# Two banded layers on one core: band products in a two-bank tile, two of eight normalised columns on VectorE, and another order of the step

## The chip, the cores and the metric

The kernel runs on one core of one Trainium2 chip. The metric is device time in microseconds (us) of one execution, as the median of several runs. The engines are named as in the profile: PE is TensorE's matmul stream, PEld its weight loads, DVE is VectorE, ACT is ScalarE, POOL is GpSimd, and SP is SyncE, which issues the DMAs.

## The reference, cut to what matters

The input `x` is 512 x 512 x 64 in float32. Two layers of the same form run one after the other, each with its own weights:

```python
def _layer(x):                       # xn: group norm of x, then layer norm over the 64 channels
    left  = (xn @ Wl + bl) * mask * sigmoid(xn @ Wlg + blg)      # 64 -> 128 channels
    right = (xn @ Wr + br) * mask * sigmoid(xn @ Wrg + brg)
    out_gate = sigmoid(xn @ Wog + bog)
    out = _banded_ingoing(left, right, 4)    # out[i,j,h] = sum over |d|<=4 of left[i+d,i,h] * right[i+d,j,h]
    out = _ln(out, out_norm_scale, out_norm_bias) * out_gate     # layer norm over the 128 channels
    return x + out @ Wo + bo
```

The sum over the band is, for each of the 128 channels, a matrix product along the first image axis with a band matrix of width 9.

## The kernel before, in words

The 512 rows are cut into nine blocks of 64 rows with some overlap, and each block into two halves of the 512 columns. A **chunk** is one block with 128 columns from each half, and the 128 partitions hold 64 rows for each of the two column halves. A layer has 18 chunks of 16 **steps**. A step `t` handles eight columns per half: one `Unit` on the input side, and, some 30 steps later, one `Out` on the output side. `RO` holds the projected right side of the chunk, and later the band products in the same place.

What a step does, by engine (the names are the functions that the loop in `layer` calls, lines 800 to 910):

- POOL: `affine` (group norm, two operations on the tile `z`, `128x512`), `inner_norm(t+2)` (subtract the mean and multiply by the inverse deviation, again two operations on `z`), the twelve small operations of the inverse square root in `solve` (every fourth step), and `biased` (adds the bias to the residual rows in `XR`). How many units are put through `affine` in a step varies: over the steps 0 to 15 of a chunk it is 1, 1, 2, 1, 2, 1, 1, 2, 1, 1, 1, 0, 1, 1, 0, 0.
- DVE: `out_stats` (statistics `sto` of the band products, from none to seven a step), `inner_stats` (statistics `sti` of `z`), the five small operations that open `solve`, `right_end` twice (writes `RO` from the projection and its gate), `times_gate` twice (writes `ZH`), `ended` (adds the residual), and one copy of band products for each call of `mix`.
- ACT: `right_gate` twice (`sg`), `gated` (`gate`, two operations), `norm` (eight operations that write `on`, four and four), `kept` (writes `zT`, two operations), and one copy of band products for each `mix`.
- PE: `right` twice (16 matmul records each), `gates`, `turned` (transposes of `on`), `transposed` (transposes of the next unit's `z`), `end` (the last projection of the step before), `sums` (statistics for the next group norm, only in the first layer), and `mix`.

`mix` computes the band product of eight channels: 16 small matmul calls (32 records in the profile) in the four 64x64 tiles of the array. Steps 0 to 9 of a chunk hold 2, 1, 2, 2, 1, 2, 1, 2, 2, 1 calls, and steps 10 to 15 hold none. Each engine works in the order in which the program issues (`InOrder`), so the order of the calls in the loop is the order of each engine's queue.

PSUM is handed out from two rings. `two_banks()` gives tiles of two banks from a ring of two buffers (`ps2`): both `right`, and `transposed`. `one_bank()` gives single banks from a ring of three in the first layer and four in the second (`ps`, `ps_all`): `gates`, `turned`, `end`, and, before the change, both halves of `mix`. A tile can be written again only when all readers of its earlier content are done. The tile `on` has one buffer, so `norm(t+1)` writes behind `turned(t)`.

Two lines say where the transposes sit before the change:

```python
            for u in inputs(t + 1):
                transposed(u)          # third use of the ps2 ring in a step: the buffer of right(units[t], 0)
```

Of the kernel before, what the change touches and what calls it, by code (L numbers as in the profile page):

```python
# [11 lines left out]
ALU = mybir.AluOpType  # L12
# [4 lines left out]
P = 128  # L17
# [5 lines left out]
JU = 8  # L23
JQ = 4
NU = JC // JU
HB = 8
HA = 16
NA = 3
NB = 32
# [24 lines left out]
def last(v: bass.AP, n: int) -> bass.AP:  # L54

    p, c = v.shape
    return v.unsqueeze(2).broadcast_to([p, c, n])
# [22 lines left out]
def tile_two_banded_layers(  # L80
# [47 lines left out]
    def one_bank():  # L128
        return ps.tile([P, 512], F32, tag="ps", name="bank")
# [302 lines left out]
    def inner_stats(u: Unit, st: bass.AP, k: int):  # L432

        en.vector.bn_stats(st[:, k, :], u.z[:, 2 * k : 2 * k + 2, :].rearrange("p t c -> p c t"))

    def inner_norm(u: Unit):
        z = u.z.rearrange("p (k t) c -> p k t c", t=2)
        m = u.mean.unsqueeze(3).broadcast_to([P, JU // 2, 2, D])
        en.gpsimd.tensor_tensor(z, z, m, ALU.subtract)
        en.gpsimd.tensor_tensor(u.z, u.z, last(u.rs, D), ALU.mult)  # L440

    def transposed(u: Unit):

# [62 lines left out]
    def right(u: Unit, q: int, w: dict):  # L506
        u.pr[q] = crossed(u, q, w["right"]).rearrange("p e k h -> p (e k) h")

    def right_gate(u: Unit, q: int):
        u.sg[q] = wk.tile([P, JQ, H], F32, tag="sg", name="sg", bufs=2)  # L510
        en.scalar.activation(u.sg[q], u.pr[q][:, :, H:], AF.Sigmoid)
# [55 lines left out]
    def mix(c: int, A: bass.AP, h0: int) -> list:  # L567


        j0 = c % 2 * (JC - JW)  # L570
        q = HB // 4
        R = RO.rearrange("p (s h) j t -> p s h j t", s=2)[:, :, h0 // 4 : h0 // 4 + q, j0 : j0 + JC]
        L = A.rearrange("p (s h) i t -> p s h i t", s=2)[:, :, h0 % HA // 4 : h0 % HA // 4 + q]
        ph = [one_bank().rearrange("i (h t j) -> i h t j", h=q, t=2) for s in range(2)]
        for h in range(q):
            for t in range(2):
                for s in range(2):
                    for e in range(2):
                        part, to = (slice(n * S, (n + 1) * S) for n in (e, e ^ s))
                        en.tensor.matmul(  # L580
                            ph[s][to, h, t, :], lhsT=L[part, s, h, :, t], rhs=R[part, s, h, :, t],
                            start=True, stop=True,
                        )
        return [(R[:, s], ph[s].rearrange("i h t j -> i h j t")) for s in range(2)]

    class Out:

# [4 lines left out]
    def out_stats(o: Out, st: bass.AP, k: int):  # L592
        en.vector.bn_stats(
            st[:, k, :],
            RO[:, :, o.c + 2 * k : o.c + 2 * k + 2, :].rearrange("p h j t -> p h t j"),
        )
# [60 lines left out]
    def gated(o: Out):  # L657
        b = o.blk
        n = 2 * JQ * b.m
        g = gp.tile([H, 4 * JQ * (S - WIN)], F32, tag="gate", name="gate")  # L660
        for e, pg in enumerate(o.pg):
            en.scalar.activation(
                g[:, e * n : (e + 1) * n].rearrange("h (k p) -> h k p", p=b.m), pg, AF.Sigmoid
            )

        o.g = g[:, : 2 * n].rearrange("h (x n p) -> h n x p", n=2, p=b.m)
# [31 lines left out]
    def biased(o: Out, w: dict, stats: bool):  # L698
        n = S + o.blk.m
        f = o.xr[:n, :, 1 : 1 + 2 * D]  # L700
        add = fewer if stats and o.blk.m < S - WIN else w["add"]
        en.gpsimd.tensor_tensor(f, f, mid(add[:n], JU // 2), ALU.add)
# [36 lines left out]
    def layer(src: bass.AP, dst: bass.AP, w: dict, stats: bool, then=None):  # L739
# [36 lines left out]
        def inputs(t: int) -> list:  # L776
            return [d[t] for d in (units, lefts) if t in d]
# [22 lines left out]
        for t in range(min(loads), last_t + 3):  # L800
            if then and t == max(units) + 2:
                then()
            for u in loads.get(t, []):
                if u not in early:
                    load(src, u)
            if t + 1 in outs:
                fetch(src, outs[t + 1], w, t + 1)
            for c, h in slabs.get(t, []):
                A[c, h] = take_left(c // per, h)
            if t + 2 in outs:  # L810
                recall(outs[t + 2])

            looking = []
            for o, k in looks.get(t, []):
                if sto is None:
                    sto = sm.tile([P, NB // 2, 6], F32, tag="sto", name="sto"), []
                st, os = sto
                if k == 0:
                    os.append(o)
                n = (len(os) - 1) * (JU // 2)  # L820
                looking.append((o, st[:, n : n + JU // 2, :], k))

            mixing, mixed = mixes.get(t, []), []
            todo = []
            for at, u in inners.get(t, []):
                key = (at + 1) // 4
                if key not in sti:
                    sti[key] = sm.tile([P, 3 * NB // 4, 6], F32, tag="sti", name="sti", bufs=3), []
                st, us = sti[key]
                n = len(us) * (JU // 2)  # L830
                u.mean = st[:, n : n + JU // 2, 1::3]
                todo += [(u, st[:, n : n + JU // 2, :], k) for k in range(JU // 2)]
                us.append(u)

            if t in lefts:
                for q in range(0, min(JU, NEAR * JQ - lefts[t].near), JQ):
                    left(lefts[t], q, w)
            for v in looking[0:3]:
                out_stats(*v)
            for u in inputs(t + 2):  # L840
                inner_norm(u)
            if t in units:
                right(units[t], 0, w)
            if t in units:
                right_gate(units[t], 0)
            if t in outs:
                gates(outs[t], w)
            if t in units:
                right(units[t], JQ, w)
            for u in affines.pop(t, []):  # L850
                affine(u, en.vector if u.at < NU + 4 else en.gpsimd)
            if t % 4 == 0 and t > NU:
                then_affine = affines.pop(t + 1, [])
            for v in looking[3:5]:
                out_stats(*v)
            for v in looking[5:]:
                out_stats(*v)
            for v in todo:
                inner_stats(*v)
            if t % 4 == 0:  # L860
                st, us = sti.pop((t + 4) // 4, (None, []))
                so, os = sto or (None, [])
                sto = None
                if us or os:
                    solve(w, us, os, st, so)
            if t in outs:
                gated(outs[t])
            if t in units:
                right_end(units[t], 0)
            if t in outs:  # L870
                biased(outs[t], w, stats)
            if t in outs:
                turned(outs[t], w)
            if t in units:
                right_gate(units[t], JQ)
            for u in inputs(t + 1):
                transposed(u)
            if t in outs:
                times_gate(outs[t], w)
            for u in then_affine:  # L880
                affine(u, en.gpsimd)
            then_affine = []
            if t - 1 in outs:
                end(outs[t - 1], w)
            if t in units:
                right_end(units[t], JQ)
            if len(mixing) > 0:
                c, h0 = mixing[0]
                mixed.append(mix(c, A[c, h0 // HA], h0))
            if t + 1 in outs:  # L890
                norm(outs[t + 1], 0, 4)
            for u in inputs(t + 1):
                kept(u)
            if stats and t - 2 in outs:
                sums(outs[t - 2], t - 2 == first_t, t - 2 == last_t)
            if len(mixing) > 0:
                en.scalar.copy(*mixed[0][0])
            if t - 1 in outs:
                ended(dst, outs[t - 1])
            if t + 1 in outs:  # L900
                norm(outs[t + 1], 4, 8)
            if len(mixing) > 1:
                c, h0 = mixing[1]
                mixed.append(mix(c, A[c, h0 // HA], h0))
            if len(mixing) > 0:
                en.vector.tensor_copy(*mixed[0][1])
            if len(mixing) > 1:
                en.scalar.copy(*mixed[1][0])
            if len(mixing) > 1:
                en.vector.tensor_copy(*mixed[1][1])  # L910

# [135 lines left out]
```

## Time and profile before

| | |
|---|---|
| median of 3 runs | 4813.95 us (4808.51 to 4821.8) |
| profiled execution: its own time | 4808.51 us |
| its span, first to last instruction | 4806.5 us |
| mean granted TensorE clock | 0.948 |
| busy, share of the span | DVE 82%, PE 79%, POOL 79%, ACT 77% |
| steps with everything at work, first layer | 16 chunks between about 555 and 2397 us |
| the same, second layer | 16 chunks between about 2842 and 4681 us |

The start of the span is the pass for the first group norm's statistics, the stretch around 2500 to 2800 us is the change of layers, and the rest is the two long stretches of the table, in which the steps repeat with the period of a chunk. Shares over the whole span mix these stages, so the step is read from windows inside the long stretches. An operation's time in the listing is from its start to its end; on DVE and ACT the next operation starts some 0.09 us before the last one's end, so sums of work are made from start to start.

### The profile page before, as it was taken

What the parts mean: (1) busy time and instruction counts of PE and PEld (TensorE: products, weight loads), DVE (VectorE), ACT (ScalarE), POOL (GpSimd) and SP (SyncE); (2) the same over time, 40 slices, a digit from 0 to 9 for tenths busy, and PEclk for the clock granted to TensorE, in tenths of its full rate; (3) what the DMA queues carried; (4) which work ended last, traced back from release to release, by engine and by line L of the source; (5) the groups of instructions that cost most, each with busy time, mean ns of one, the idle gap of its engine ahead of it and who ended that gap; (6) DMA issues with size and microseconds to landing.
All of it is one profiled execution on the core that took longest, in us unless ns stands there. A gap on an engine that the chain in (4) does not pass through costs nothing. (4 is left out here: it accounts for less than half of the span.)

```text
span 4806.5 us, 193543 instructions
## 1 busy us (share of the span) xinstructions
PE 3796.6 (79%) x76306; PEld 3293.0 (69%) x76306; DVE 3929.9 (82%) x9635; ACT 3708.4 (77%) x8732; POOL 3817.1 (79%) x4739
## 2 busy tenths in 40 slices
PE   1025799989999999999985478888888888888888
PEld 0024688878888887888854467777777777777775
DVE  6954788888888888888867478888888888888887
ACT  0013689888888898989883268888888888888899
POOL 0035999999999999999734589999999999999964
PEclk9997999999999999999997689999999999999999
DMA  7859677777777777777763967777777777777876
GB/s 299 336 178 108 172 212 213 215 210 215 211 209 210 211 214 212 214 212 215 199 170 100 105 168 212 216 214 209 217 213 215 213 213 218 210 216 211 222 200 179
DMA packets 1437651, 983.63 MB, mean 205 GB/s; under 512 B 167202, under 2 KB 1284424, under 8 KB 1432392
## 3 DMA queue, kind: packets, MB, share of 16 engines
q1 hardware_dynamic: 1432064, 969.75, 73.6%
q8 instruction: 604, 9.90, 0.9%
q14 instruction: 303, 2.48, 0.2%
q10 hardware_dynamic: 4680, 1.50, 0.1%
HBM read 658.42 MB, written 312.46 MB: 202 GB/s over the span
## 5 line engine op out<-in xcount | busy, mean ns | idle before, releaser
L373 ACT ACTIVATE on<-RO,nm,rs 128x128 f32<-128x128 f32 x4608 | 1927.7, 496 | 15.3 <-PE bank L373 9.9
L373 PEld LDWEIGHTS banks<-pack,zT 64*128 64x128 f32 x18576 | 1251.3, 195 | 549.5 <-ACT zT L373 288.9
L373 PE MATMUL banks<-pack,zT 64*128 64x128 f32 x18576 | 1365.6, 289 | 272.8 <-ACT zT L373 222.6
L373 DVE TENSOR_TENSOR RO<-banks,sg 128x512 f32<-128x512 f32 (+1 forms) x1188 | 795.3, 673 | 228.3 <-POOL sg L373 116.2
L373 DVE SCALAR_TENSOR_TENSOR ZH<-bank,pack,gate 128x448 f32<-128x448 f32 (+1 forms) x1152 | 741.6, 685 | 173.3 <-PE bank L373 97.3
L373 ACT ACTIVATE sg<-banks 128x512 f32<-128x512 f32 (+1 forms) x1188 | 698.0, 589 | 188.6 <-PE banks L373 188.2
L373 DVE BATCH_NORM_STATS2 sto<-RO 128x6 f32<-128x256 f32 x2304 | 800.8, 411 | 3.7
L373 POOL TENSOR_TENSOR z<-z,gb 128x512 f32<-128x512 f32 x536 | 684.8, 1278 | 42.0
L373 PE MATMUL bank<-RO,A 64*64 64x128 f32 x18432 | 706.0, 292 | 3.9 <-ACT RO L373 2.4
L373 PE MATMUL bank<-pack,ZH 128*64 128x64 f32 x18432 | 694.6, 231 | 5.0 <-ACT gate L373 4.1
L373 POOL TENSOR_TENSOR z<-z,ga 128x512 f32<-128x512 f32 x536 | 685.6, 1279 | 3.2 <-DMA z<-mid_x 1.9
L373 POOL TENSOR_TENSOR z<-z,rs 128x512 f32<-128x512 f32 x586 | 619.3, 1057 | 46.0
L373 DVE COPY RO<-bank 128x512 f32<-128x512 f32 x576 | 398.4, 692 | 310.6 <-PE bank L373 307.3
L373 PEld LDWEIGHTS bank<-pack,ZH 128*64 128x64 f32 x18432 | 612.6, 143 | 47.3 <-ACT gate L373 8.5
L373 POOL TENSOR_TENSOR z<-z,sti 128x512 f32<-128x512 f32 x586 | 627.9, 1072 | 0.0
L373 PEld LDWEIGHTS bank<-RO,A 64*64 64x64 f32 x18432 | 582.0, 142 | 43.0 <-ACT RO L373 4.1
L373 ACT ACTIVATE gate<-bank 128x448 f32<-128x448 f32 (+1 forms) x1152 | 565.8, 545 | 34.5 <-PE bank L373 32.0
L373 ACT ACTIVATE zT<-banks 128x512 f32<-128x512 f32 (+1 forms) x1084 | 463.5, 481 | 139.6 <-PE banks L373 128.9
L373 PE MATMUL bank<-zg,pack 64*128 64x448 f32 (+1 forms) x2304 | 564.3, 556 | 4.6 <-DMA zg<-later 4.6
L373 ACT COPY RO<-bank 128x512 f32<-128x512 f32 x576 | 333.2, 579 | 282.3 <-PE bank L373 282.1
L373 PE MATMUL banks<-ident,z 64*128 64x64 f32 x4336 | 254.1, 233 | 359.2 <-DVE RO L373 336.9
L373 DVE BATCH_NORM_STATS2 sti<-z 128x6 f32<-128x128 f32 x2344 | 500.5, 280 | 15.2 <-POOL z L373 14.2
(144 smaller groups left out, 3908.6 us busy)
## 6 DMA issues: line engine op xcount, KB each, us to landing
later<-zT SPq DMA_DIRECT2D x576, 256.0 KB
A<-left_of SPq DMA_DIRECT2D x1152, 128.0 KB
zg<-later SPq DMA_DIRECT2D x576, 256.0 KB
z<-in_x_dram SPq DMA_DIRECT2D x576, 128.0 KB
z<-mid_x SPq DMA_DIRECT2D x576, 128.0 KB
gn_x<-in_x_dram SPq DMA_DIRECT2D x16, 4096.0 KB
XR<-in_x_dram SPq DMA_DIRECT2D x448, 112.0 KB
mid_x<-XR SPq DMA_DIRECT2D x448, 112.0 KB
```

The lines of the kernel that those rows point to most:

```text
L373: return lambda *a, **k: tc.keep_in_program_order(f(*a, **k))
```

## The change

Three things are changed. `mix` takes one tile of two banks in place of two tiles of one bank, with the same matmuls and the same copies. For units behind number 16, `inner_norm` on POOL handles six of the eight columns, and the new `inner_norm_v` does the other two on DVE, one `tensor_scalar` of `128x64` per column, which subtracts and multiplies at once with two per-partition scalars. And the calls of a step come in another order: by engine, before and after:

| engine | before | after |
|---|---|---|
| PE | right 0, gates, right 4, turned, transposed, end, mix, sums, mix | gates, right 0, right 4, turned, end, sums, transposed, mix, mix |
| ACT | right_gate, gated, right_gate, norm 0-4, kept, copy, norm 4-8, copy | gated, right_gate, right_gate, norm 0-4, kept, copy, copy, norm 4-8 |
| DVE | stats, solve, right_end, times_gate, right_end, ended, copy, copy | stats, solve, right_end, right_end, times_gate, inner_norm_v, ended, copy, copy |
| POOL | inner_norm, affine, solve, biased, affine of the next step | affine, inner_norm, solve, biased, affine of the next step |

```diff
+ZV = 2
...
     def inner_norm(u: Unit):
-        z = u.z.rearrange("p (k t) c -> p k t c", t=2)
-        m = u.mean.unsqueeze(3).broadcast_to([P, JU // 2, 2, D])
-        en.gpsimd.tensor_tensor(z, z, m, ALU.subtract)
-        en.gpsimd.tensor_tensor(u.z, u.z, last(u.rs, D), ALU.mult)
+        n = ZV if u.at > NU else 0
+        m = last(u.mean.rearrange("p k t -> p (k t)")[:, n:], D)
+        en.gpsimd.tensor_tensor(u.z[:, n:], u.z[:, n:], m, ALU.subtract)
+        en.gpsimd.tensor_tensor(u.z[:, n:], u.z[:, n:], last(u.rs[:, n:], D), ALU.mult)
+
+    def inner_norm_v(u: Unit):
+        for j in range(ZV if u.at > NU else 0):
+            en.vector.tensor_scalar(
+                u.z[:, j], u.z[:, j], u.mean[:, j // 2, j % 2 : j % 2 + 1], u.rs[:, j : j + 1],
+                ALU.subtract, ALU.mult,
+            )
...
-        ph = [one_bank().rearrange("i (h t j) -> i h t j", h=q, t=2) for s in range(2)]
+        pb = two_banks()
+        ph = pb.rearrange("i (s h t j) -> i s h t j", s=2, h=q, t=2)
...
-                            ph[s][to, h, t, :], lhsT=L[part, s, h, :, t], rhs=R[part, s, h, :, t],
+                            ph[to, s, h, t, :], lhsT=L[part, s, h, :, t], rhs=R[part, s, h, :, t],
```

The rest of the diff moves the calls in the loop of `layer` (lines 835 to 910), as in the table. The calls that issue DMAs (`fetch`, `take_left`, `recall`, `kept`, `ended`) keep their order on SP's queue.

More of the change, by code (lines that the diff above doesn't have):

```diff
@@ L580, in mix @@
                         en.tensor.matmul(
-                            ph[s][to, h, t, :], lhsT=L[part, s, h, :, t], rhs=R[part, s, h, :, t],
+                            ph[to, s, h, t, :], lhsT=L[part, s, h, :, t], rhs=R[part, s, h, :, t],
                             start=True, stop=True,
                         )
-        return [(R[:, s], ph[s].rearrange("i h t j -> i h j t")) for s in range(2)]
+        return [(R[:, s], ph[:, s].rearrange("i h t j -> i h j t")) for s in range(2)]
     class Out:
@@ L837, in layer @@
                     left(lefts[t], q, w)
[L838 to L845, printed above, removed]
             if t in outs:
@@ L848, in layer @@
             if t in units:
-                right(units[t], JQ, w)
+                right(units[t], 0, w)
             for u in affines.pop(t, []):
@@ L853, in layer @@
                 then_affine = affines.pop(t + 1, [])
-            for v in looking[3:5]:
+            if t in units:
+                right(units[t], JQ, w)
+            if t in outs:
+                gated(outs[t])
+            if t in units:
+                right_gate(units[t], 0)
+            for v in looking[0:2]:
                 out_stats(*v)
-            for v in looking[5:]:
+            for u in inputs(t + 2):
+                inner_norm(u)
+            for v in looking[2:5]:
                 out_stats(*v)
@@ L859, in layer @@
                 inner_stats(*v)
+            if t in outs:
+                turned(outs[t], w)
+            for v in looking[5:]:
+                out_stats(*v)
             if t % 4 == 0:
@@ L865, in layer @@
                     solve(w, us, os, st, so)
+            if t in units:
+                right_gate(units[t], JQ)
             if t in outs:
-                gated(outs[t])
+                biased(outs[t], w, stats)
             if t in units:
                 right_end(units[t], 0)
[L870 to L873, printed above, removed]
             if t in units:
-                right_gate(units[t], JQ)
-            for u in inputs(t + 1):
-                transposed(u)
+                right_end(units[t], JQ)
             if t in outs:
                 times_gate(outs[t], w)
+            if t + 1 in outs:
+                norm(outs[t + 1], 0, 4)
+            if t - 1 in outs:
+                end(outs[t - 1], w)
+            for u in inputs(t + 2):
+                inner_norm_v(u)
             for u in then_affine:
@@ L882, in layer @@
             then_affine = []
[L883 to L886, printed above, removed]
+            if stats and t - 2 in outs:
+                sums(outs[t - 2], t - 2 == first_t, t - 2 == last_t)
+            for u in inputs(t + 1):
+                transposed(u)
             if len(mixing) > 0:
@@ L889, in layer @@
                 mixed.append(mix(c, A[c, h0 // HA], h0))
-            if t + 1 in outs:
-                norm(outs[t + 1], 0, 4)
             for u in inputs(t + 1):
                 kept(u)
-            if stats and t - 2 in outs:
-                sums(outs[t - 2], t - 2 == first_t, t - 2 == last_t)
             if len(mixing) > 0:
                 en.scalar.copy(*mixed[0][0])
[L898 to L901, printed above, removed]
             if len(mixing) > 1:
@@ L904, in layer @@
                 mixed.append(mix(c, A[c, h0 // HA], h0))
+            if len(mixing) > 1:
+                en.scalar.copy(*mixed[1][0])
+            if t - 1 in outs:
+                ended(dst, outs[t - 1])
             if len(mixing) > 0:
                 en.vector.tensor_copy(*mixed[0][1])
-            if len(mixing) > 1:
-                en.scalar.copy(*mixed[1][0])
+            if t + 1 in outs:
+                norm(outs[t + 1], 4, 8)
             if len(mixing) > 1:
```

## The prediction

> **What bounds the kernel now.** I read the busy shares first, then the stage windows, the costliest groups by form inside a window, the waits, and last the timeline of single steps. The stage windows give the two long stretches (columns: us, then busy us of PE, PEld, DVE, ACT, POOL):
>
> ```profile
> 555.00:2397.00 1842.00, 1685.28 (x35737) 1486.35 (x35729) 1575.02 (x3863) 1645.50 (x3830) 1668.90 (x2020) 0.98 0.76 211
> 2842.00:4681.00 1839.00, 1555.13 (x32030) 1361.09 (x32028) 1631.69 (x3903) 1619.22 (x3870) 1677.51 (x2041) 0.96 0.77 213
> ```
>
> No engine is far from full. Timed between the first gate activations of corresponding steps in the timeline, a chunk of 16 steps takes 115.6 us in layer 1 and 114.4 us in layer 2, mean 115.0. Scaled to a chunk, PE is busy 105.8 and 96.8 us, ACT 103.3 and 100.7, DVE 98.8 and 101.5. For POOL the groups by form (1300 to 1900 us) give the sum:
>
> ```profile
> L373 POOL TENSOR_TENSOR z<-z,gb 128x512 f32<-128x512 f32 x84 | 107.4, 1278 | 6.6
> L373 POOL TENSOR_TENSOR z<-z,ga 128x512 f32<-128x512 f32 x83 | 106.2, 1279 | 0.0
> L373 POOL TENSOR_TENSOR XR<-XR,fewer 120x512 f32<-120x512 f32 x83 | 98.6, 1188 | 0.3 <-DMA XR<-in_x_dram 0.2
> L373 POOL TENSOR_TENSOR z<-z,sti 128x512 f32<-128x512 f32 x82 | 86.6, 1056 | 0.0
> L373 POOL TENSOR_TENSOR z<-z,rs 128x512 f32<-128x512 f32 x82 | 85.5, 1043 | 6.4
> ```
>
> Sixteen steps of these five are 16 x 5.844 = 93.5 us. A `solve` occupies POOL for 4.56 us from its first small operation to its last (1309.61 to 1314.17 in the timeline), four of them 18.2. Together 111.7 of 115.6: POOL is the bound, and most of the rest is its wait for DVE at the four solves.
>
> The timeline of step 4 of a chunk in layer 2 (that step took 11.7 us, an ordinary one 5.7 to 8.0) shows the second thing that matters (start, duration; DVE, POOL, then PE):
>
> ```profile
> 3671.69 0.99 DVE L373 TENSOR_SCALAR var<-sti 128x32 f32<-128x32 f32 x1
> 3672.61 0.18 DVE L373 SCALAR_TENSOR_TENSOR var<-sto,pack 128x32 f32<-128x32 f32 x1
> 3672.83 1.20 DVE L373 TENSOR_SCALAR var<-var 128x32 f32<-128x32 f32 x1
> 3673.94 0.17 DVE L373 TENSOR_SCALAR nm<-sto 128x32 f32<-128x32 f32 x1
> 3674.06 1.23 DVE L373 TENSOR_SCALAR rs<-var 128x64 int32<-128x64 int32 x1
> ...
> 3671.38 1.27 POOL L373 TENSOR_TENSOR z<-z,ga 128x512 f32<-128x512 f32 x1
> 3672.73 1.26 POOL L373 TENSOR_TENSOR z<-z,gb 128x512 f32<-128x512 f32 x1
> 3673.95 1.29 POOL L373 TENSOR_TENSOR z<-z,ga 128x512 f32<-128x512 f32 x1
> ...
> 3676.03 0.46 PE L373 MATMUL banks<-ident,z 64*128 64x64 f32 x8 [3.91 <-DVE RO L373]
> 3676.43 1.97 PE L373 MATMUL bank<-pack,ZH 128*64 128x64 f32 x32
> ```
>
> A DVE `tensor_scalar` from SBUF to SBUF ends about 0.04 us after the POOL operation that was running when it started: 0.99, 1.20 and 1.23 us, where with POOL idle the same ones take 0.17, 0.18 and 0.20. The one that follows a blocked one directly (`nm<-sto`) took 0.17 and slipped in ahead of POOL's next operation. And PE stood 3.91 us, because `transposed` waits for `right_end`, behind the solve on DVE; its matmuls then ran slower (32 in 1.97 us, elsewhere 1.15).
>
> **The change part by part.**
>
> *POOL, inner_norm on six columns.* Two operations lose 128 of 512 elements each. In proportion that is 0.26 us each; by the slope between `128x64` (0.32) and `128x512` (1.05) it is 1.6 ns x 128 = 0.21. So 0.42 to 0.52 us a step; I take 0.45, 7.2 a chunk: POOL falls to 104.5, plus the 3.9 it waits now, 108.4. With that it stops being the bound unless everything else is cheap.
>
> *DVE, two new tensor_scalar of 128x64.* The nearest row has the same shape and a per-partition scalar, with POOL idle, at the change of layers:
>
> ```profile
> L935 DVE TENSOR_SCALAR on<-same,on x2: 256/256/256, 2561.3 to 2561.7; 128x64 f32<-128x64 f32 x2
> ```
>
> The next DVE operation starts 0.09 us before the end of one, so two cost 2 x 0.17 = 0.34 us of DVE's queue. The first also waits for the POOL operation it meets. A POOL operation of length d is met in proportion to d and leaves d/2: per chunk 16 x (2 x 1.28² + 2 x 0.84² + 1.19²)/2 = 49, over a period near 112, is 0.44, with the small ones 0.46 us. Bounds for the first wait are nothing (POOL idle) and 1.28 (it just started). For the second I take nothing, as for `nm<-sto`, which took 168 to 181 ns in the 137 of its 144 runs that lie in the two layers' steps (median 174, once 1251 in the rest); its other end is a whole further POOL operation, 0.84 to 1.28. So 0.80 us a step, 12.8 a chunk. Behind the new pair on DVE queue `ended`, the copies of the band products and the next step's statistics; the buffers of `right` and `RO` wait on those.
>
> *DVE as the new bound.* From start to start, the timeline gives about 0.60 us for each `right_end`, `times_gate` half, `ended` and copy (96 a chunk: 57.6), 0.33 for a piece of output statistics (64: 21.1), 0.20 for one of input statistics (64: 12.6) and 0.65 for the start of a solve (2.6): 94. From busy time less blocked tensor_scalar it is 96.6. I take 95. With 12.8 it is 107.8. The tensor_scalar of the solves wait 0.56 us a solve now in layer 1 (means 0.49 and 0.41 for `var<-sti` and `var<-var`) and 1.2 in layer 2; with POOL less behind I take 0.6, 2.4 a chunk. Two more for steps in which another engine is last: step 14 has few statistics (DVE 4.1 + 0.8 against ACT's 5.7), and with two `mix` ACT's second copy now waits for a matmul group whose buffer `kept` must free. Sum 112.2 us, above PE and ACT in both layers.
>
> *Order on PE.* `end` (1.15 us) and in layer 1 `sums` (0.69) go ahead of `transposed`, so the wait for `right_end` is covered by them: 64.6 us per 600 in layer 2 (waits view, `PE banks <- DVE RO`), 37.9 in layer 1. On the path this is worth nothing by itself while DVE is last, but it takes away the pauses in which ACT and DVE stand for PE, and I count DVE's present 13 to 16 us of idle time a chunk as gone but for those two us. This is the boldest step.
>
> *mix in the two-bank ring.* Same matmuls, same copies: no work. It frees the single-bank ring, and makes `right` of the next step wait for the copies of the band products. Between the last copy and the `right_end` that needs the projection DVE has statistics and the first `right_end`, 1.3 + 0.8 + 0.6 = 2.7 us, and the matmuls, the sigmoid and the hand-overs need some 1.9, so it is covered; without that cover it would cost up to 1.9 us in each of five steps.
>
> *POOL and SP queues.* `affine` now stands ahead of `inner_norm(t+2)`, which comes 2.6 to 5.1 us later, but is needed by PE a step later: nothing. SP issues in the same order: nothing.
>
> *Sum.* 115.0 - 112.2 = 2.8 us a chunk, 32 chunks: 90 us. The profiled execution took 4808.5 (span 4806.5), so 4718.5; the median of the runs lies 5.4 above it: **4724 us**. The ends of the stages and the change of layers are left as they are.
>
> On the second tensor_scalar a rule speaks against me. The Trainium skill (SBUF — State Buffer, "Who interferes with whom") says that VectorE in a two-port mode and GpSimd share one port pair by an exclusive lock, which the first holds for its whole instruction while the other blocks. Read strictly, POOL's waiting operation takes the pair between the two, and the sum would be that of rival 1; the `nm<-sto` rows show one exception, without per-partition scalars.
>
> **The rivals.**
>
> 1. *The second tensor_scalar is blocked too.* Then it loses a POOL operation whenever the first met one that is followed at once by an independent one (`gb`, the multiply, `biased`: (1.28 + 0.84 + 1.19) x 16 of a period near 119, 0.45), each about 1.1 us: 0.48. With 0.43 for the first, the pair costs 1.25 a step: 95 + 20 + 4.4 = 119.4, 4.4 us a chunk more, 141 us: **4955 us, slower**. It decides from 0.98 us a step for the pair (0.80 + 2.8/16). For it: per-partition scalars may start later than `nm<-sto` did, and `rs<-var`, 0.12 us behind that, was blocked for 1.23. Against: the 137 passes.
> 2. *The pair hardly waits*, because POOL, ahead now, idles or runs the small operations of a solve. At 0.34 a step DVE needs some 102; POOL's 108.4 bounds: 6.6 x 32 = 211 us less, **4600 us**. Against: POOL is still busy over nine tenths.
> 3. *The ring binds.* If the cover of the copies is gone, 5 x 1.9 = 9.5 us a chunk, 304 us: **5030 us**. For it: DVE is late more often; against: the statistics that stand between.
> 4. *Nothing gained or lost*: the pair near 0.98 us, **4810 us**.
>
> **How the numbers follow.** Forecast 0.38 (its own range 4640 to 4790), rival 1 0.31, rival 2 0.11, rival 3 0.10, rival 4 0.10. The range reaches from the better end, 4605, to 5000, which takes in most of rival 1 and leaves out the far half of rivals 2 and 3. A measurement of this kernel tells about 0.3% (14 us) from no change. Faster: 0.38 + 0.11 + 0.01 = 0.50; same 0.06; slower 0.31 + 0.10 + 0.03 = 0.44.
>
> **What would show it.** Right: POOL busy near 104 us a chunk, DVE over 95% busy in the long stretches, the new `z<-z` tensor_scalar of DVE at a mean near 0.7 us for the first and 0.26 for the second, PE's wait for `RO` before the transposes mostly gone, chunks near 112 us. Rival 1 shows as second tensor_scalar of over 0.8 us in a third or more of the steps; rival 2 as both near 0.26; rival 3 as PE `banks` waiting for the copies `RO`. If DVE has more than 5 us of idle time a chunk, the step on the order is wrong.

## The result and the profile after

The changed kernel takes 4837.32 us (median of 4 runs, 4828.45 to 4842.72), the kernel before beside it 4813.48 us (4 runs). The ratio is 1.0046 with the interval [1.0025, 1.0067]: slower by about half a per cent. The forecast was 4724 us, faster. The profiled execution took 4837.08 us, with a span of 4835.3.

The stage windows of after, with the columns of the prediction's first view (us, then busy us of PE, PEld, DVE, ACT, POOL):

```profile
555.00:2397.00 1842.00, 1681.31 (x35569) 1451.98 (x35568) 1788.46 (x4358) 1644.17 (x3807) 1567.83 (x2023) 1.00 0.76 211
2842.00:4681.00 1839.00, 1602.79 (x31643) 1336.66 (x31640) 1796.08 (x4375) 1630.73 (x3823) 1569.46 (x2028) 0.99 0.76 211
```

DVE went from 1575 and 1632 us to 1788 and 1796, that is 97 and 98% of the windows; POOL fell by 101 and 108 us. DVE is the bound now, as forecast, but with more work than forecast: a chunk takes 116.3 us in layer 1 and 115.8 in layer 2 (before 115.6 and 114.4, forecast 112.2).

The groups by form of after (1300 to 1900 us; busy us, mean ns of one, idle before) show the columns that moved:

```profile
L374 DVE TENSOR_SCALAR z<-z,sti,rs 128x64 f32<-128x64 f32 x164 | 97.9, 638 | 0.0
...
L374 POOL TENSOR_TENSOR z<-z,sti 128x384 f32<-128x384 f32 x82 | 69.2, 844 | 0.0
L374 POOL TENSOR_TENSOR z<-z,rs 128x384 f32<-128x384 f32 x82 | 68.6, 837 | 6.4
```

POOL's two operations shrank from 1056 and 1043 ns to 844 and 837. What they gave is 0.42 us a step; the 164 new operations of DVE, two a step, have a mean of 638 ns each. The spread of one of them is in the answer by tile (min, median, max in ns):

```profile
L374 DVE TENSOR_SCALAR z<-z,sti,rs x164: 300/462/1331, 1303.7 to 1895.2; 128x64 f32<-128x64 f32 x164
```

The floor is 300 ns here, and the median lies above it: at least half of them wait. The timeline shows for what. First DVE's rows of three steps (start, duration; the `x2` row is the pair, the row behind it is `ended`), then POOL's rows at those times:

```profile
3656.46 1.95 DVE L374 TENSOR_SCALAR z<-z,sti,rs 128x64 f32<-128x64 f32 x2
3658.33 0.68 DVE L374 TENSOR_TENSOR XR<-bank,XR 120x512 f32<-120x512 f32 x1
...
3671.26 2.00 DVE L374 TENSOR_SCALAR z<-z,sti,rs 128x64 f32<-128x64 f32 x2
3673.18 0.68 DVE L374 TENSOR_TENSOR XR<-bank,XR 120x512 f32<-120x512 f32 x1
...
3702.29 0.87 DVE L374 TENSOR_SCALAR z<-z,sti,rs 128x64 f32<-128x64 f32 x2
3703.08 0.68 DVE L374 TENSOR_TENSOR XR<-bank,XR 120x512 f32<-120x512 f32 x1
...
3656.29 1.27 POOL L374 TENSOR_TENSOR z<-z,gb 128x512 f32<-128x512 f32 x1
3657.52 0.84 POOL L374 TENSOR_TENSOR z<-z,sti 128x384 f32<-128x384 f32 x1
...
3671.23 0.83 POOL L374 TENSOR_TENSOR z<-z,rs 128x384 f32<-128x384 f32 x1
3672.02 1.19 POOL L374 TENSOR_TENSOR XR<-XR,pack 120x512 f32<-120x512 f32 x1
...
3702.05 0.83 POOL L374 TENSOR_TENSOR z<-z,sti 128x384 f32<-128x384 f32 x1
3702.96 0.89 POOL L374 TENSOR_TENSOR z<-z,rs 128x384 f32<-128x384 f32 x1
```

At 3656.46 the first `tensor_scalar` meets `gb`, which ends at 3657.56. POOL's next operation had started at 3657.52, before that end, and the second `tensor_scalar` waits for it as well: the pair ends at 3658.41, 0.05 us behind it. At 3671.26 the same happens with the multiply and `biased`. At 3702.29 POOL's next operation is the multiply, which needs the result of the subtract and starts 0.08 us after its end; there the second gets through, and the pair takes 0.87 us.

Over all steps of the two windows, from start to start in the timeline, the first of the pair takes 0.49 us, the second 0.62 (layer 1) and 0.67 (layer 2), the pair 1.11 and 1.17, mean 1.14. The floor is 0.22 each. Half of the first ones and 51 and 57% of the second ones last over 0.4 us; all of these second ones last over 0.8 us, which the prediction gave as the sign of rival 1 ("in a third or more of the steps").

Two readings of the waits of after, between 3400 and 4000 us (us in total, times, longest):

```profile
PE banks L374 <- DVE RO L374: 67.6, 78, 1.8
...
PE bank L374 <- DMA zg<-later: 7.1, 8, 1.7
```

In total PE's wait for `RO` is not gone (64.6 us before, 55 times); its longest fell from 3.9 to 1.8 us. But it is now two waits, which the instruction records tell apart: the transposes waiting for `right_end`, all of the 64.6 us before, are down to 36.8, and the other 30.8 are new: the matmuls of `right` wait for DVE's copies of band products, whose two-bank buffer they need. The second line is new as well: the gates' input `zg`, which `recall` loads, lands late. Before, no wait of PE in this window ended on it (in all of layer 2's long stretch one, of 0.4 us).

### The profile page after: what moved, and what is told of

The parts are those of the page before. It is cut to its first block, busy times and chain, and to the rows that moved or that the text cites. A ratio compares the mean times of both kernels' runs of the same rounds, so it can differ in the third digit from the quotient of the medians.

```text
span 4835.3 us, 193356 instructions
## 1 busy us (share of the span) xinstructions
PE 3858.8 (80%) x76306; PEld 3246.6 (67%) x76306; DVE 4360.2 (90%) x10719; ACT 3745.5 (77%) x8732; POOL 3599.2 (74%) x4739
## 4 chain that ended last, share of the span: by engine, by line
PE 39%; DVE 30%; DMA 11%; POOL 6%; issue 5%; ACT 5%; SPq 3%; ACTq 0%; DVEq 0%; POOLq 0%
PE banks L374 20%; PE bank L374 19%; DVE RO L374 8%; DVE z L374 6%; DVE ZH L374 5%; ACT on L374 3%; POOL z L374 3%; SPq L374 3%; DVE gn_st L374 3%; DVE sto L374 3%; DMA zg<-later 2%; DVE XR L374 2%; DVE sti L374 2%; DMA mid_x<-XR 1%; POOL rsqrt L374 1%
## 5 line engine op out<-in xcount | busy, mean ns | idle before, releaser
L374 ACT ACTIVATE on<-RO,nm,rs 128x128 f32<-128x128 f32 x4608 | 1928.5, 499 | 16.1 <-PE bank L374 12.7
L374 DVE TENSOR_TENSOR RO<-banks,sg 128x512 f32<-128x512 f32 (+1 forms) x1188 | 753.1, 672 | 242.6 <-ACT sg L374 119.5
L374 ACT ACTIVATE sg<-banks 128x512 f32<-128x512 f32 (+1 forms) x1188 | 666.3, 594 | 280.4 <-PE banks L374 274.1
L374 PE MATMUL bank<-zg,pack 64*128 64x448 f32 (+1 forms) x2304 | 724.9, 595 | 71.4 <-DMA zg<-later 43.4
L374 PE MATMUL banks<-RO,A 64*64 64x128 f32 x18432 | 632.2, 281 | 37.8 <-DVE RO L374 6.5
L374 DVE TENSOR_SCALAR z<-z,sti,rs 128x64 f32<-128x64 f32 x1084 | 657.1, 647 | 0.0
L374 PEld LDWEIGHTS banks<-RO,A 64*64 64x64 f32 x18432 | 531.4, 136 | 89.4 <-DVE RO L374 68.7
L374 POOL TENSOR_TENSOR z<-z,rs 128x384 f32<-128x384 f32 (+1 forms) x586 | 508.1, 867 | 45.9
L374 PE MATMUL bank<-ident,on 64*128 64x64 f32 x9216 | 473.6, 227 | 49.3 <-ACT gate L374 39.4
L374 POOL TENSOR_TENSOR z<-z,sti 128x384 f32<-128x384 f32 (+1 forms) x586 | 512.8, 875 | 0.0
L374 POOL TENSOR_TENSOR XR<-XR,pack 120x512 f32<-120x512 f32 (+1 forms) x352 | 417.2, 1188 | 121.3 <-DMA XR<-mid_x 51.5
```

Source lines behind the costliest of these rows:

```text
L374: return lambda *a, **k: tc.keep_in_program_order(f(*a, **k))
```

## The experiments

Each run stands beside runs of the kernel before on the same chip, where that took 4836 to 4839 us; so ratios are compared, not times. Chunk lengths are for layer 1 / layer 2. Edits are to the kernel after unless told otherwise.

**No column on DVE**, so that only the order and the two-bank `mix` are left:

```diff
-ZV = 2
+ZV = 0
```

> The new order and the two-bank ring for the band products alone: no column is normalised on DVE, inner_norm on POOL has all eight again. Theory A (DVE sets the time of the changed kernel: its 95 us of work a chunk, 16 pairs of tensor_scalar that wait for POOL's operations, 3 us idle): POOL is the bound again at 111.7 us a chunk plus 2 to 3.3 us of waits, so 114 to 115 us a chunk, 4780 to 4813 us, a ratio of 0.993 to 1.000 to the kernel before. Theory B (the order, or the ring that makes right wait for the copies, costs time, and the two columns on DVE win some of it back): slower than the changed kernel, above 4850 us.

Measured: 4814.4 us, 0.9954 [0.9937, 0.9971], chunks 114.5 / 114.0. The order and the ring together bring about half a per cent, and the columns take it back with interest. The ratio lies in the range expected. What DVE saves on the pair it loses in part on other operations, as the groups by form of this run show (2842 to 4681 us; in the kernel after the same two have means of 265 and 161 ns):

```profile
L374 DVE TENSOR_SCALAR var<-var 128x32 f32<-128x32 f32 x65 | 56.2, 864 | 2.2
L374 DVE TENSOR_SCALAR var<-sti 128x32 f32<-128x32 f32 x63 | 32.1, 510 | 0.0
```

Without the pair the `tensor_scalar` of the solves wait longer for POOL; with `rs<-var` (378 ns against 196) the three take 1.1 us more a solve, some 4.5 us a chunk.

**One column on DVE:**

```diff
-ZV = 2
+ZV = 1
```

> One column on DVE in place of two, the rest as changed. Theory A: only the first wait is left, some 0.28 us, with 0.22 us of own time 0.5 us a step: DVE 95 + 8 + 3 = 106 us a chunk; POOL is relieved of half as much, 111.7 - 3.3 = 108.4, and waits 3.3: 111.7 us a chunk, 4705 us, ratio 0.977. Theory B: about midway between the changed kernel and e1, which is slower: 4840 us or more.

Measured: 4818.58 us, 0.9960 [0.9947, 0.9974], chunks 115.5 / 114.9. A miss (0.977 was expected): the one `tensor_scalar` took 0.50 and 0.51 us from start to start, as the first of the pair does (0.49), but the chunk hardly followed. The waits show 45 us in layer 2 in which PE waits for `zg`; that became a theory of its own, D: once DVE has time to spare, the late load of `zg` sets the length of steps 10 to 13.

**The two columns apart**, one before `times_gate` and one behind it:

```diff
+            for u in inputs(t + 2):
+                inner_norm_v(u, 0)
             if t in outs:
                 times_gate(outs[t], w)
...
             for u in inputs(t + 2):
-                inner_norm_v(u)
+                inner_norm_v(u, 1)
```

> The two tensor_scalar of a step are set apart, the first ahead of times_gate and the second behind it. Theory A with the second operation losing the race for the port when it follows the first at once (second: 0.70 us mean, first 0.58): both wait as a first one does, 2 x 0.5 = 1.0 us a step against 1.14 in the changed kernel, 2.2 us a chunk less, 70 us: 4767 us, ratio 0.99. If the wait does not depend on what stands ahead of the operation (rival C: every tensor_scalar waits 0.4 us, wherever it stands), no change against the changed kernel, 4837 us.

Measured: 4841.4 us, 1.0020 [1.0004, 1.0035], chunks 116.3 / 114.1. On DVE the two now cost 0.44 + 0.50 and 0.41 + 0.51 us, 0.93 together against 1.14. In time little of it arrives: the ratio expected was 0.99, and the interval overlaps that of the change, as rival C had it. Step 11 of a chunk, timed from gates to gates, grew to 7.8 / 7.6 us (after 6.8 / 6.5), and in step 12 DVE idles 0.9 / 0.8 us (after 0.2 / 0.1). That fits gates that come late for want of `zg`, for which PE waits 50 us in layer 2; the same edit was run again below with `zg` earlier.

**An operation without the wait** in place of the pair, so that DVE keeps something of its length and POOL keeps its relief. It leaves two columns of each later unit unnormalised:

```diff
-            en.vector.tensor_scalar(
-                u.z[:, j], u.z[:, j], u.mean[:, j // 2, j % 2 : j % 2 + 1], u.rs[:, j : j + 1],
-                ALU.subtract, ALU.mult,
-            )
+            en.vector.bn_stats(idle, u.z[:, :2].rearrange("p t c -> p c t"))
```

> Each of the two tensor_scalar is replaced by a bn_stats of 128x128 over the same two columns into an unused tile, an operation with one input and a result of six numbers, of 0.20 us from start to start, 0.39 us for the two; the two columns are then not normalised at all, so the subtraction and the product are left out for a quarter of the values. Theory A: DVE has nearly the same own work (0.44 us a step in the changed kernel) but no wait for POOL: 95 + 6 + 3 = 104 us a chunk, POOL 104.9 + 3.3 = 108.2 is the bound, 6.8 us a chunk below the kernel before, 4595 us, ratio 0.955. Theory B (order or ring): little gain, above 4780 us.

Measured: 4787.33 us, 0.9903 [0.9878, 0.9927], chunks 114.1 / 113.0; so without the pair's waits at POOL some 1.4% of the changed kernel's time is gone (0.9903 against 1.0046), but the 4.5% below the kernel before that were expected did not come. The waits of this run in layer 2 (2842 to 4681 us) name what came next:

```profile
PEld bank L375 <- DMA zg<-later: 99.8, 67, 4.0
...
PE bank L375 <- DMA zg<-later: 87.4, 61, 3.8
```

In the kernel after the second row has 19.4 us. In steps 7, 8 and 11 to 13 the load of `zg` is issued 5.3 to 9.7 us ahead of the first matmul of the gates before the change, 3.8 to 5.9 after it, and 3.4 to 5.0 here (medians over a layer's chunks). Where the gates' weight load waits for it in layer 2, that ends 2.9 to 5.3 us behind the issue here, with a median of 3.4. `recall` stands on SP's queue behind `fetch` and `take_left`, and the issues of a step with a slab load take SP about 7 us.

**`recall` first on SP's queue**, with the change otherwise as it is:

```diff
+            if t + 2 in outs:
+                recall(outs[t + 2])
             # ... the loads of the step ...
-            if t + 2 in outs:
-                recall(outs[t + 2])
```

> The changed kernel with one call moved: recall(t+2), the load of zg, is issued first in a step, ahead of the loads of z, of XR and of A. In the changed kernel the gates' matmuls, now first on PE, stand behind that load for some 1.2 to 1.6 us a chunk. Theory A (DVE with the port sets the time): DVE is idle less than 3.5 us a chunk, of which 1.4 in a step without output statistics, so at most 0.5 us a chunk is to be had: ratio to the kernel before 1.000 to 1.005, as the changed kernel. Theory D (the late loads set the time): 1.5 us a chunk and more, ratio below 0.995.

Measured: 4854.56 us, 1.0030 [1.0018, 1.0043], chunks 116.0 / 116.2. PE's wait for `zg` is gone and the time is not: with both columns on DVE the load is hidden, DVE is late anyway.

**The same two edits together** (two columns left unnormalised, as above):

> As e4 (bn_stats in place of the two tensor_scalar, so two columns of eight stay unnormalised), with recall(t+2) issued first in a step. In e4 PE waited for zg 63 us in layer 1 and 87 to 100 us in layer 2 of 16 chunks, 4 to 6 us a chunk, mostly in steps 10 to 13. Theory D (e4 fell short of its 0.955 because these loads became the next bound): 3 to 5 us a chunk less than e4, 96 to 160 us, ratio 0.957 to 0.970. Theory E (the steps with two mix calls, at 7.57 us on the chain transposed, kept, second mix, copy, and the solves bind in e4): as e4, 0.985 to 0.992.

Measured: 4718.01 us, 0.9751 [0.9737, 0.9766], chunks 112.1 / 110.7. The waits of this run in the same window:

```profile
PEld bank L375 <- DMA zg<-later: 4.0, 8, 1.5
...
PE bank L375 <- DMA zg<-later: 2.7, 4, 1.4
```

Some 85 us of PE's waiting went, and 1.5% of the time with it, where the same edit brought nothing with the pair in place. So D holds, and the waits at POOL hid it. The run still stops short of its expectation (0.957 to 0.970); steps with two `mix` stay at 7.57 us, in which ACT idles 0.7 to 0.8 us, and why was not settled.

**One column, `recall` first:**

> As e2 (one column on DVE) with recall(t+2) issued first in a step. Theory D: e2 fell short of its 0.977 for the same reason; steps 11 and 12 took 7.4 to 7.6 and 6.9 to 7.4 us there against 5.7 to 5.9 in the kernel before; 2 to 3 us a chunk less than e2, 64 to 96 us: ratio 0.976 to 0.983. Theory E: as e2, 0.994 to 0.998.

Measured: 4769.38 us, 0.9860 [0.9845, 0.9875], chunks 113.4 / 113.3. It is short of the expected 0.976 to 0.983, and why was not settled; but it does the whole computation and is the fastest such kernel of the study, 1.4% ahead of the kernel before.

**The columns in the old order**, the kernel before with `inner_norm` on six columns, `inner_norm_v` behind `times_gate`, and the single-bank `mix` as it was:

> The kernel before with only the two columns moved from POOL to DVE: its order, its single-bank mix, and inner_norm_v behind times_gate. Theory A: the pair costs DVE about 1.1 us a step, 18 a chunk; half of DVE's idle 13 to 16 us of the kernel before (waits for the band products behind transposed and end) takes some of it: DVE 95 + 18 + 6 to 8 = 119 to 121 us a chunk, 130 to 190 us slower than the kernel before, ratio 1.027 to 1.04; the new order is then what makes the changed kernel come out near 1.00. Theory B (the new order or the ring costs): faster than the changed kernel, ratio below 1.002.

Measured: 4939.3 us, 1.0212 [1.0195, 1.0228], chunks 119.5 / 117.5: slower, as expected, but by less than the 1.027 to 1.04. Its windows:

```profile
555.00:2397.00 1842.00, 1613.55 (x34506) 1406.62 (x34506) 1714.50 (x4250) 1610.17 (x3694) 1531.58 (x1972) 0.99 0.74 205
2842.00:4681.00 1839.00, 1513.47 (x30732) 1300.61 (x30726) 1735.85 (x4302) 1603.03 (x3693) 1564.49 (x2010) 0.98 0.74 206
```

The pair costs 1.05 us here too, and DVE still idles 8.1 / 6.2 us a chunk in which it waits for others; in the new order that is 3.3 / 2.7. So the columns by themselves are the loss, and the new order with its ring wins 1.6% of it back.

**The columns apart, `recall` first:**

> e3 (the two tensor_scalar set apart by times_gate) with recall(t+2) issued first. In e3 the two took DVE 0.44 and 0.50 us from start to start in layer 1, 0.41 and 0.51 in layer 2, together 0.93 against 1.11 and 1.17 in the changed kernel, 3 to 4 us a chunk less, but step 11 grew to 8.0 and 7.7 us, where PE waits for zg. Theory F (what the split saves on DVE was given back to the late load): 2 to 4 us a chunk less than the changed kernel, 64 to 128 us, ratio to the kernel before 0.978 to 0.991. Rival C (the place of the two does not matter to the time): as e3 and the changed kernel, 1.000 to 1.005.

Measured: 4802.62 us, 0.9933 [0.9909, 0.9957], chunks 115.4 / 113.0: 0.9% below the split pair without that edit, though a little short of the expected 0.978 to 0.991. DVE's idle time in step 12 is down to 0.1 us. Two columns are faster than the kernel before once they cost 0.93 us instead of 1.14 and `zg` comes in time.

**No column, `recall` first:**

> e1 (new order, two-bank mix, no column on DVE) with recall(t+2) issued first. Theory A: POOL's 111.7 us a chunk plus 1 to 2 us of waits is the floor, 112.7 to 113.7 against 114.0 to 114.5 in e1: 25 to 50 us less than e1, ratio 0.985 to 0.991. If it comes out below e7 (0.986), then no column on DVE is worth its price in this order.

Measured: 4781.56 us, 0.9883 [0.9869, 0.9898]. Against it one column is worth 0.2%, and the intervals overlap.

**The single-bank `mix` in the new order**, to see whether the two-bank ring costs anything (theory E). First on the kernel with `bn_stats` in place of the pair, then on the one with one column, both with `recall` first:

```diff
-        pb = two_banks()
-        ph = pb.rearrange("i (s h t j) -> i s h t j", s=2, h=q, t=2)
+        ph = [one_bank().rearrange("i (h t j) -> i h t j", h=q, t=2) for s in range(2)]
```

> e6 (bn_stats in place of the two tensor_scalar, two columns of eight unnormalised, recall first) with mix in two single banks as before the change: the part of the change that concerns the banks, alone. In e6 steps with two mix calls take 7.57 us with 0.7 to 0.8 us of ACT idle, by the chain transposed, kept, second mix, copy. Theory E (that ring costs): these steps fall to 6.8 to 7.2 in layer 2, where PE has room, four of them 1.5 to 3 us a chunk less in layer 2, ratio 0.967 to 0.972. Rival (DVE, idle 0.03 to 0.6 us in the same steps, or the smaller ring of single banks, takes it back): as e6, 0.973 to 0.978, or slower.

Measured: 4840.22 us, 1.0006 [0.9996, 1.0015], against 0.9751 with two banks.

> e7 (one column on DVE, recall first) with mix in two single banks as before the change. Theory A: in e7 DVE is idle 0.0 to 0.4 us in the steps with two mix calls, so a shorter chain there frees nothing: as e7, 0.984 to 0.988. Theory E (the ring costs): 1 to 3 us a chunk less, 0.976 to 0.982.

Measured: 4877.57 us, 1.0080 [1.0064, 1.0097], against 0.9860. E falls twice, and by more than it promised in the other direction: in the new order the two-bank tile is worth 2.2 to 2.6%. ACT's wait for the band products, first of this run and then of its two-bank counterpart, both in layer 2:

```profile
ACT RO L374 <- PE bank L374: 170.1, 235, 2.3
```

```profile
ACT RO L374 <- PE banks L374: 105.7, 193, 1.2
```

Steps with two `mix` take 8.3 to 9.1 us with single banks and 7.6 with the two-bank tile (steps 2, 3 and 7 of a chunk): `gates`, `turned`, `end` and four halves of `mix` then share the small ring. Most of the loss lies in layer 1, where that ring has three banks and not four: chunks of 117.8 / 112.7 us after 112.1 / 110.7, and 118.6 / 113.9 after 113.4 / 113.3.

The ratios by columns on DVE, all in the new order with the two-bank tile:

| on DVE | `recall` as in the change | `recall` first |
|---|---|---|
| none | 0.9954 | 0.9883 |
| one column | 0.9960 | 0.9860 |
| two, apart | 1.0020 | 0.9933 |
| two, as a pair (the change) | 1.0046 | 1.0030 |
| `bn_stats` for the pair (two columns left out) | 0.9903 | 0.9751 |

## Why the prediction was wrong, step by step

**The failed step is the price of the pair**, above all the second `tensor_scalar`, which was taken at nothing behind its own length. It waited 0.42 us a step on average. The own time was mis-sized too, 0.44 us for the two and not 0.34 (the row taken as nearest lasted 256 ns, these some 300 and more), and the first wait was smaller, 0.28 and not 0.46. Together 1.14 against 0.80, and the text had put the point from which it decides at 0.98. The runs bear that out from both sides: 1.14 gives 1.0046, and split to 0.93 the two give 1.0020, and 0.9933 with `zg` in time. So rival 1's mechanism was the right one, at a smaller size (1.14, not 1.25). That the time came near rival 4's is luck, a balance of errors: a chunk is 3.9 us longer than forecast, 5.4 of it from the pair and 1.0 from idle time, less 1.6 that the solves and 0.9 that the rest of DVE's work took less.

**Why the second waits** is seen by sorting the pairs of the whole trace by the POOL operation that runs when the first starts and by the time from its end to the start of POOL's next one (pairs whose first meets at least 0.05 us of that operation):

| POOL's operation, and its next | pairs | POOL's next starts | second over 0.4 us |
|---|---|---|---|
| `ga`, then `gb` (dependent) | 40 | 0.08 us after the end | 2.5% |
| small operations of `solve` | 131 | | 2% |
| subtract, then multiply (dependent) | 79 | 0.08 us after | 41% |
| `gb`, then subtract | 66 | 0.04 us before the end | 98% |
| `biased`, then `ga` | 75 | 0.04 us before | 100% |
| `biased`, then subtract | 35 | | 100% |
| multiply, then `biased` | 44 | 0.04 us before | 100% |

Where POOL's next operation needs nothing of the last, it has started before DVE's second can. Behind a first that was blocked, the second starts 0.02 to 0.03 us before the end of POOL's operation: 0.01 to 0.03 us too late where POOL's next one is ready, 0.1 us in time where it is not. At 3657 us, in the rows above, the records to the nanosecond say that POOL's subtract starts at 3657.520, the second `tensor_scalar` at 3657.535, and `gb` ends at 3657.564. The row with 41% comes apart by the first's start. The 47 that got through had at least 0.26 us of the subtract still to run; there the first ends 0.05 us behind it, and the second starts before the multiply. The 32 that did not had less than 0.20 us: there the first takes its own 0.30 us, and the second starts 0.03 to 0.17 us behind the subtract's end, when the multiply is at hand.

The prediction reasoned from `nm<-sto`, which got through 137 times, and what it held for rival 1 ("per-partition scalars may start later than `nm<-sto` did") was the point. Behind a blocked `var<-var` in the long stretches of before (47 times) `nm<-sto` starts 0.042 to 0.047 us before the end of POOL's operation, 0.015 us earlier than the new pair's second. In 16 of the 47 POOL's next operation was independent and started within 0.007 us of `nm<-sto`, mostly just behind it; `nm<-sto` got through every time. In the prediction's own rows it starts at 3673.942 (to the nanosecond), POOL's `ga` at 3673.949. In the other 31 POOL's next operation came 0.12 us behind it or later. Why the new `tensor_scalar` starts later, for its per-partition scalars or for another difference, was not tested.

The rule of the Trainium skill (SBUF — State Buffer, "Who interferes with whom") held here on DVE's side: a blocked `tensor_scalar` ends 0.05 us after POOL's operation. The page says that the pair of ports goes to whoever issues first, and the order of starts above agrees, but for six of the 32 blocked in the 41% row, which started ahead of the multiply, five by 0.01 us or less and one by 0.05. On POOL's side the records show less than a full block: a multiply that starts while a `tensor_scalar` of DVE has some 0.2 us still to run takes 0.89 us (median of 67), against 0.83 with none (315).

**What held.** POOL's relief, 0.42 us against 0.45 taken. POOL no longer the bound: its five operations are 5.43 us a step now, 86.9 a chunk, with 18.2 for the solves 105.1 (forecast 104.5). DVE as the new bound. The idle time of DVE, called the boldest step: 3.3 / 2.7 us a chunk against 2 forecast and 16.5 / 12.7 before. The solves' waits fell, to some 1.1 / 0.4 us a chunk from their means, where 2.4 was taken. With these the sum closes: 18.2 for sixteen pairs, 0.75, 3.0, and the 116.05 measured leave 94.1 for the base, of which 95 was forecast.

**The cover under two zeros was thinner than told.** "SP issues in the same order: nothing" and the gates ahead of `right` at no price are right for the change as it stands (`recall` first brings nothing there), but only because DVE is late: in every version in which DVE is relieved, the late `zg` takes 0.7 to 1.5%. Had the pair cost 0.80, the forecast would still have been missed for this reason: the run without the pair's waits stood at 0.9903 with `recall` where the change has it, and 4724 is 0.981 of 4813.95. The order on SP was the same; the gates' place in the step had moved towards it.

**The rivals.** Rival 2 (the pair hardly waits) is what the run without the pair's waits shows, where with `zg` in time 4718.01 us came out against 4838.76, 121 of the 211 us that it named. Rival 3 (the ring binds) has its sign in the trace: in the long stretches of after the matmuls of `right` on PE stand 70.2 us in layer 1 and 90.3 in layer 2 for DVE's copies of band products, and never before the change. But they wait for the engine that is the bound. What can come back to DVE is its wait for the gate `sg` (layer 1, then layer 2, 16 chunks each):

```profile
DVE RO L374 <- ACT sg L374: 42.6, 53, 2.3
DVE RO L374 <- ACT sg L374: 28.8, 27, 2.3
```

That is 2.7 and 1.8 us a chunk at most, against the 9.5 that the rival named, and before the change it was 32.3 and 34.5 us. As a whole the two-bank tile is a gain of 2.2 to 2.6% in this order, in the two versions in which it was taken back (with the pair itself it was not), and in the prediction it was given no gain at all.

**The parts of the change**, then: two columns on DVE cost 2.1% in the old order; the new order and the two-bank tile together bring 0.5% without columns; and of the two the tile is needed, since with single banks neither version in the new order was faster than the kernel before (1.0006 and 1.0080). Single banks without columns were not run.

## What to carry to other kernels

Before moving a two-input operation from POOL to DVE, write down for each place in DVE's queue which POOL operation it meets and whether POOL's next one is independent: here a `tensor_scalar` cost the rest of the running operation, and a second one right behind it cost the whole next operation if that was ready. An operation that gets through in such a place today is no proof for another: `nm<-sto` did by starting 0.015 us earlier. One such operation per place, with others between, was cheaper than a pair (0.93 us against 1.14). And when a move lets an engine go, ask at once which transfer was hidden behind its lateness: here a load that cost nothing in the changed kernel took 1.5% of the one that was rid of the pair's waits.

## What the runs showed of the hardware

- A `tensor_scalar` of `128x64` with two per-partition scalars took some 300 ns at the least (0.22 us from start to start), while the one with a single scalar in the change of layers took 256.
- An operation of POOL that does not depend on the one before it starts 0.04 us before that one's end in the records, a dependent one 0.08 us after it. A second `tensor_scalar` behind a blocked one starts 0.02 to 0.03 us before that end, so this decides whether it gets in: it was blocked in all 193 cases with an independent next operation, and got through in 65 of 67 in which `ga` was followed by `gb` or the subtract by the multiply.
- With no columns on DVE some of the wait at POOL shows up elsewhere: the solve's `var<-var` then had a mean of 864 ns in layer 2 (520 with `bn_stats` in place of the pair, 265 with the pair). What sets its place was not tested.
